# Second slot-routing FFN of a macaron block: its routing written as a table of pieces, emitted among the last stages of the attention, with its transposes done by DMA

## The chip, the cores and the metric

One NeuronCore of a Trainium2 chip runs the whole kernel. The metric is the device time of one execution in microseconds (us); lower is better. A core has five engines that work side by side, each on its own in-order queue: TensorE (PE, matrix products and transposes into PSUM), VectorE (DVE), ScalarE (ACT), GpSimd (POOL) and SyncE (SP, which here only issues transfers). Sixteen DMA engines move data between HBM and the on-chip memory SBUF; SP and ACT issue to them. An engine that waits holds up everything behind it on its queue.

## The reference

Two batches of 4096 tokens with 512 features go through three residual parts, each on a layer norm of its input:

```python
x = x + 0.5 * ffn(layernorm(x))
x = x + attn(layernorm(x))
x = x + 0.5 * ffn(layernorm(x))
```

The attention is a gated delta rule with 16 heads of 32: a 32 x 32 state per head that each token decays, corrects and reads, then an RMS norm, a SiLU gate and an output product. The FFN routes tokens to 64 slots, and the same weights serve both times:

```python
h = gelu(concat(x, mean(S)) @ w1.T + b1)                 # 256 hidden
logits = (h @ w2.T + b2) / (abs(tau) + 0.1)              # 64 slots
alpha = top8_softmax(logits)                             # dense [token, slot], 8 nonzero
slot_input = einsum('bts,btd->bsd', alpha, x) / alpha.sum(1)
S_new = gru(slot_input, S)                               # on 2 x 64 slots only
out = einsum('bts,bsd->btd', alpha, S_new @ wv.T + bv) @ wo.T + bo
```

So an FFN has three stages: a routing over all tokens, a small GRU that needs the routing of every token, and a pass over all tokens that adds alpha times the slot values.

## The kernel before

Tokens are worked on in 32 blocks of 128 positions, both batches together (tiles [128, 2, 512]). The stages in order of time:

1. `ffn_a_phase(..., "a", ...)`: first routing, with the weights' preparation among it, then the first GRU.
2. `attention(...)`: per block, the first FFN's closing product, layer norm, q/k/v/gate projections, triangular solve, a chunked recurrence (`chain`, four chunks of 32 tokens a block, lines 1001 to 1045), and `tail` (norm, gate, output product, residual add at L1083, store to `x2d` in HBM).
3. `ffn_a_phase(..., "c", ...)`: second routing and second GRU (`gru`, L510 on).
4. `after_c`: the closing pass, which adds the second FFN's output to x2 (L641) and stores the result (L642).

The attention is software-pipelined by hand. Each stage of a block is a Python generator that yields after a piece of work, and the table `PIPE` says, in one long line of words such as `chain.2` or `qk0.5*2`, which generator is advanced next and by how many blocks it runs ahead of the loop's step. `run_pipe` walks the table for k from minus the largest lead to 31, under `tc.manual_schedule()`, so each engine gets its instructions in the order of emission. `chain`, `vload`, `tload` and `tail` have leads of 0 to 3; all other stages have done block 31 when step k = 28 ends. The last three steps hold only the recurrence and the tails of the last blocks: the drain.

A routing works on groups of blocks. `split_blocks` makes groups of 1, 4 x 7, 2 and 1 blocks. For each group six generators are entered with start and end times from `PA`, merged by time in `run_merged`, and then ordered by the framework's own scheduler:

- `a_load` loads an x2 block of 512 KB on SP (`load_x2`, L602). The last KEEP = 12 blocks go to tiles that stay until the closing pass (`kx`), the others to XT = 4 rotating tiles (`xt`).
- `a_stats` takes mean and variance on VectorE (L361, L362), then square root (ACT, L365) and reciprocal.
- `a_norm` normalises on VectorE into `xn` (L379, two buffers), casts the high half to fp16 on ScalarE (`xh`, L383), and subtracts on GpSimd for the low half (`xl`, L385). TensorE transposes both halves, 8 + 8 transposes of 128 x 128 into PSUM (L394). ScalarE copies the high half out (`xTh`, L397) and VectorE the low half (`xTl`, L399).
- `a_hidden` makes the hidden layer, 24 matmuls of 256 columns a block (`mm3`, L128 to L130), Gelu on ScalarE (L417), and the logits (L421).
- `a_topk` finds the top 8 of 64 on VectorE with an exponential on ScalarE (L431 to L458) and sums alpha on GpSimd (L461).
- `a_slots` transposes alpha (L472), stores it on chip through `alpha_keep` (L595), and accumulates the slot inputs in PSUM (L480 to L482).

Memory is taken from pools that are opened and closed like a stack. Before, the second routing's pools are opened after the attention's pools and its weights (`aw_es.close()`) are closed. In PSUM (8 banks) the attention holds 2 banks for transposes (`a1t`), 3 for projections (`a1p`), 1 for `pa` and 2 for `pc`.

After the second GRU's weights, 11 x2 tiles (F3X) are loaded for the closing pass; the remaining 9 are loaded in it, on ScalarE's queue (L616).

Of the kernel before, what the change touches and what calls it, by code (L numbers as in the profile page):

```python
# [9 lines left out]
F32 = mybir.dt.float32  # L10
F32R = mybir.dt.float32r
F16 = mybir.dt.float16
# [7 lines left out]
P = 128  # L20
D = 512
# [13 lines left out]
HEAD, TAIL = 1, 1  # L35
CFG = {"a": dict(XT=7, XN=2, XH=10), "c": dict(XT=4, XN=2, XH=11)}
KEEP = 12
F3A, F3X, F3L = 4, 11, 8
# [14 lines left out]
def split_blocks(n):  # L53

    cuts = [0] + list(range(HEAD, n - TAIL, GB)) + [n - TAIL, n]
    cuts = sorted(set(cuts))
    return [(a, b - a) for a, b in zip(cuts, cuts[1:])]
# [17 lines left out]
def run_pipe(tc, stages, n):  # L75


    order = []
    for w in PIPE.split():
        w, _, m = w.partition("*")  # L80
        name, lead = w.split(".")
        order += [(name, int(lead))] * int(m or 1)
    live = {}
    with tc.manual_schedule():
        for k in range(-max(lead for _, lead in order), n):
            for name, lead in order:
                t = k + lead
                if 0 <= t < n:
                    if (name, t) not in live:
                        live[name, t] = stages[name](t)  # L90
                    next(live[name, t], None)
# [3 lines left out]
def tile_macaron(  # L95
# [87 lines left out]
    aw = aw_es.enter_context(tc.tile_pool(name="aw", bufs=1))  # L183
    W = {}
    for n_, cols, dt in (("wqh", NQ, F16), ("wql", NQ, F16), ("wgh", 2 * D, F16), ("wgl", 2 * D, F16),
                         ("wo", D, F32)):
        W[n_] = aw.tile([P, KC, cols], dt, tag=n_, name=n_)
# [121 lines left out]
    def ffn_a_phase(load, adst, nm, extra, before=None, after=None):  # L309

        with tc.tile_pool(name=f"sl{nm}", bufs=1, space=PSUM) as slp, tc.tile_pool(name=f"gp{nm}", bufs=1) as gp:
# [3 lines left out]
            with tc.tile_pool(name=f"f{nm}", bufs=2) as wp, tc.tile_pool(name=f"fs{nm}", bufs=2) as sm, \  # L315
# [3 lines left out]
                groups = split_blocks(NBLK)  # L319
# [4 lines left out]
                for g, (b0, n) in enumerate(groups):  # L324
# [3 lines left out]
                        (t0 - PA["ld"] - n / GB, t1 - PA["ld"] - n / GB, lambda a=args: a_load(*a, load)),  # L328
                        (t0 - PA["st"], t0 - PA["st"] + PA["std"], lambda a=args: a_stats(*a)),
                        (t0, t1, lambda a=args: a_norm(*a)),  # L330
                        (t0 + PA["a2"], t1 + PA["a2"], lambda a=args: a_hidden(*a)),
                        (t1 + PA["a2"], t1 + PA["tk"], lambda a=args: a_topk(*a, wacc)),
                        (t1 + PA["tk"], t1 + PA["tk"] + PA["sl"] * n / GB, lambda a=args: a_slots(*a, adst, sl, ng)),
# [5 lines left out]
            with ExitStack() as es:  # L339
# [3 lines left out]
                if before:  # L343
                    before(es)
                gru(gr, sl, wacc[:, 0:NB], gw, nm)
                if after:
                    after()
# [820 lines left out]
```

## Time and profile before

| | us |
|---|---|
| Median of 3 runs (2350.8 to 2357.18) | 2355.56 |
| The profiled execution, time | 2342.8 |
| The profiled execution, span of the trace | 2341.0 |

| Stage, read from the trace | from (us) | to (us) |
|---|---|---|
| First routing and first GRU | 0 | 303 |
| Attention, to its last solve (L993) | 303 | 1960 |
| Attention, drain to the last residual add (L1083) | 1960 | 2003 |
| Second routing | 2003 | 2250 |
| Second GRU | 2250 | 2283 |
| Closing pass | 2283 | 2341 |

Over the whole span TensorE is busy 90%, VectorE 82%, ScalarE 49% and GpSimd 35%. These are means over stages of very different kinds, so the stages are read one by one: a row of busy times gives, for a stretch of time, each engine's busy us and in brackets its instructions, then the clock that was granted to TensorE (1.00 is full), the busy share of the 16 DMA engines and the GB/s they moved. A line of the timeline gives start, duration, engine, line of the kernel, operation, output and inputs; in square brackets is the idle time of the engine just before, and what ended it. A group line adds count, total busy us, mean ns of one, and the idle time before its instructions. Busy times of TensorE include overlap of pipelined matmuls.

### The profile page before, as it was taken

To read this page: it belongs to the slowest core of one execution; us is meant where nothing else is said; L and a number is where in the kernel's file an instruction comes from. 1 tells how busy PE (TensorE), PEld (TensorE's weight loads), DVE (VectorE), ACT (ScalarE), POOL (GpSimd) and SP (SyncE) were. 2 spreads that over 40 slices of the span, in tenths; PEclk is the share of its full clock that TensorE was granted. 3 is DMA by queue.
4 is the path that set the end of the run, shared out by engine and by line. 5 is a ranking of instruction groups with operands and counts; after the bars stand their busy time and mean duration, and the time that the engine had idled before them with its cause. 6 is when DMAs were issued, how large, how long until landed. Compare 5 with 4: busy or idle time off the path is not lost. (4 is left out here: it accounts for less than half of the span.)

```text
span 2341.0 us, 101047 instructions
## 1 busy us (share of the span) xinstructions
PE 2100.5 (90%) x44989; PEld 1585.4 (68%) x44989; DVE 1911.3 (82%) x4876; ACT 1148.9 (49%) x1957; POOL 808.5 (35%) x750
## 2 busy tenths in 40 slices
PE   5878878999999999999999999999999976588886
PEld 5767757767777676777767677777667754377774
DVE  7898538988888888888889888888888886489656
ACT  4677445544445444444545444554444421367631
POOL 2333114433334343333434333444333441134300
PEclk9898989999999999999999999999999988799997
DMA  6332323344443344343334444344444332630049
GB/s 212 123 127 91 96 87 129 119 133 130 142 134 126 123 136 132 128 150 121 126 124 139 128 136 148 120 127 132 135 128 146 102 97 70 219 110 29 2 149 368
DMA packets 176516, 302.75 MB, mean 129 GB/s; under 512 B 27984, under 2 KB 73552, under 8 KB 176080
## 3 DMA queue, kind: packets, MB, share of 16 engines
q1 hardware_dynamic: 161728, 256.45, 32.9%
q10 hardware_dynamic: 14352, 39.85, 5.2%
q8 instruction: 352, 5.77, 1.2%
q14 instruction: 84, 0.69, 0.1%
HBM read 189.23 MB, written 107.00 MB: 127 GB/s over the span
## 5 line engine op out<-in xcount | busy, mean ns | idle before, releaser
L1080 PE MATMUL apo<-wo,Gt 128*128 128x512 f32 x512 | 279.1, 630 | 24.5 <-DVE x1r L1083 24.5
L128 PE MATMUL pv<-xTh,wgh 128*128 128x256 f16 x1024 | 282.1, 275 | 0.0
L129 PE MATMUL pv<-xTh,wgl 128*128 128x256 f16 x1024 | 280.2, 274 | 0.1
L130 PE MATMUL pv<-xTl,wgh 128*128 128x256 f16 x1024 | 280.3, 274 | 0.0
L1014 POOL TENSOR_TENSOR ps<-ST,AC 128x256 f32<-128x256 f32 x128 | 105.5, 824 | 442.4 <-DVE ST L1038 442.4
L128 PE MATMUL pq<-wqh,xTh 128*128 128x384 f16 (+1 forms) x768 | 242.8, 316 | 1.5 <-issue 0.8
L129 PE MATMUL pq<-wqh,xTl 128*128 128x384 f16 (+1 forms) x768 | 240.9, 314 | 0.2 <-DVE xTl L818 0.2
L130 PE MATMUL pq<-wql,xTh 128*128 128x384 f16 (+1 forms) x768 | 240.7, 313 | 0.0
L862 POOL TENSOR_TENSOR qk<-qk,rn 128x512 f32<-128x512 f32 x128 | 137.6, 1075 | 231.7 <-issue 106.7
L836 ACT ACTIVATE qk<-pq,iscA 128x384 f32<-128x384 f32 (+1 forms) x192 | 105.4, 549 | 162.5 <-PE pq L130 139.5
L980 POOL TENSOR_TENSOR KQ<-KQ,Ax 128x512 f32<-128x512 f32 x128 | 168.4, 1315 | 0.4 <-PE pa L959 0.4
L764 DVE TENSOR_TENSOR tmp<-N,MT 128x256 f32<-128x256 f32 (+7 forms) x384 | 161.2, 426 | 5.6
L758 DVE TENSOR_TENSOR tmp<-N,U 128x256 f32<-128x256 f32 (+7 forms) x384 | 164.0, 434 | 1.4
L838 ACT ACTIVATE sq<-pq,iscA 128x384 f32<-128x384 f32 (+1 forms) x192 | 164.7, 858 | 0.0
L1018 PEld LDWEIGHTS pc<-KQ,S 32*32 32x32 f32 x8192 | 123.2, 106 | 50.6 <-ACT Y L1044 31.0
L760 DVE TENSOR_REDUCE MT<-tmp 128x32 f32<-128x256 f32 (+7 forms) x384 | 153.8, 407 | 0.0
L959 PE MATMUL pa<-KQ 32*32 32x64 f32 x8192 | 143.6, 217 | 11.2 <-ACT KQ L872 4.9
L1018 PE MATMUL pc<-KQ,S 32*32 32x64 f32 x8192 | 142.8, 217 | 9.5 <-DVE S L1040 4.9
L959 PEld LDWEIGHTS pa<-KQ 32*32 32x32 f32 x8192 | 121.7, 105 | 37.9 <-issue 14.9
L1035 PEld LDWEIGHTS pc<-X,u 32*32 32x32 f32 x8192 | 120.7, 105 | 38.6 <-issue 21.9
L1035 PE MATMUL pc<-X,u 32*32 32x64 f32 x8192 | 141.9, 216 | 5.2 <-ACT u L1032 3.7
L917 ACT ACTIVATE vg<-pv,iscA 128x512 f32<-128x512 f32 x128 | 88.1, 688 | 96.7 <-PE pv L130 88.7
(304 smaller groups left out, 5760.3 us busy)
## 6 DMA issues: line engine op xcount, KB each, us to landing
d<-a0d ACTq DMA_DIRECT2D x32, 528.0 KB
Ax<-a0d ACTq DMA_DIRECT2D x32, 528.0 KB
xt<-in_x_dram SPq DMA_DIRECT2D x32, 512.0 KB
x<-in_x_dram SPq DMA_DIRECT2D x64, 256.0 KB
x1d<-x SPq DMA_DIRECT2D x64, 256.0 KB
vtd<-vg SPq DMA_DIRECT2D x64, 256.0 KB
kd<-qk SPq DMA_DIRECT2D x64, 256.0 KB
XK<-kd SPq DMA_DIRECT2D x256, 64.0 KB
```

What stands on the lines that cost most here:

```text
L128: nc.tensor.matmul(po, lh, rh, start=start, stop=False, skip_group_check=True)
L129: nc.tensor.matmul(po, ll, rh, start=False, stop=False, skip_group_check=True)
L130: nc.tensor.matmul(po, lh, rl, start=False, stop=stop, skip_group_check=True)
L758: V.tensor_tensor(tv, vw(f, o10 + j0, [[C, n], [0, h], [1, ni]]), vw(U, ou + j0 * 17, [[0, n], [16, h], [1, ni]]), ALU.mult)
L760: yield lambda tv=tv, j0=j0: V.tensor_reduce(vw(mt, n * j0, [[1, n], [n, h]]), tv, AX.X, ALU.add)
L764: V.tensor_tensor(tv, vw(f, o11 + r0 * C, [[C, h], [0, n], [1, nk]]), vw(mt, 0, [[0, h], [n, n], [1, nk]]), ALU.mult)
L838: nc.scalar.activation(sq[:, f0:f1].rearrange("p (q g e) -> p q e g", g=NG, e=C), pq[:, 0:f1 - f0].rearrange("p (q e g) -> p q e g", g=NG, ...
L959: nc.tensor.matmul(pa[s, m], KQ[s, 0, c, b, g], KQ[s, :, c, b, g], start=(m == 0), stop=True, skip_group_check=True, tile_position=(32 * q ...
L980: nc.gpsimd.tensor_tensor(kc, kc, bass.AP(Ax.tensor, Ax[:, :, c].offset, [list(a[0]), [1, 2], list(a[1]), [1, C]]), ALU.mult)
L1018: nc.tensor.matmul(pcv[s, b, g, 0:2 * C], S[s, b, g], KQ[s, :, c, b, g], start=(g == 0), stop=False, skip_group_check=True, tile_position=tp)
L1035: nc.tensor.matmul(pcv[s, b, g, C:3 * C], u[s, b, g], d["X"][s, :, m], start=False, stop=True, skip_group_check=True, tile_position=tp)
L1080: nc.tensor.matmul(po, Gt[:, k, b], wo[:, k], start=(k == 0), stop=(k == KC - 1))
```

## The change

The second routing gets its own functions; the first keeps the old ones, renamed `fa_...` and `first_routing`. Five things are done:

- A table `ROUTE` orders the second routing's pieces, as `PIPE` orders the attention's, and its emission is fixed by hand. `run_pipe` is split so that a walk through a table (`pieces`) can be advanced step by step.
- When the attention's loop reaches its drain (`now >= drain`, the step after k = 28), the pools of its early stages (`ee`) and its projection weights are closed, `open_c` opens the second routing in that memory, and the walk through `ROUTE` is advanced among the attention's last pieces, from its first step (k = -4) up to `AHEAD` = 1.0 at the attention's end. The rest of the walk follows the attention.
- In `a_norm` two transposing DMA transfers a block, issued on SP, take the place of the TensorE transposes and of the copies out of PSUM. The normalisation is done in place in the `xt` tile, except for the kept blocks.
- The x2 loads are issued on ScalarE's queue. Pools are opened with `reuse_waits="tile"`, by which a new tile waits for the users of the tiles it lies on, not for the whole old pool. The three projection banks of PSUM are shared by attention and routing, which has one bank each for alpha's transposes, logits and slots.
- Numbers: groups of 1, 3, 4 x 6, 3 and 1; XT 6 for 4, XH 8 for 11; KEEP 11 for 12, F3X 12 for 11, F3L 9 for 8.

```diff
-HEAD, TAIL = 1, 1
-CFG = {"a": dict(XT=7, XN=2, XH=10), "c": dict(XT=4, XN=2, XH=11)}
-KEEP = 12
-F3A, F3X, F3L = 4, 11, 8
+HEAD, TAIL = (1, 4), (4, 1)
+CFG = {"a": dict(XT=7, XN=2, XH=10), "c": dict(XT=6, XH=8)}
+KEEP = 11
+
+AHEAD = 1.0
+F3A, F3X, F3L = 4, 12, 9
...
+def pieces(stages, n, table, extra=()):
+
+
+
+    order = leads(table)
+    live = {}
+    heap = [(s0, i, None) for i, (s0, s1, f) in enumerate(extra)]
+    heapq.heapify(heap)
+
+    def others(now):
+        while heap and heap[0][0] <= now:
+            _, i, g = heapq.heappop(heap)
+            s0, s1, f = extra[i]
+            g = g or f()
+            try:
+                heapq.heappush(heap, (s0 + next(g) * (s1 - s0), i, g))
+            except StopIteration:
+                pass
+
+    for k in range(-max(lead for _, lead in order), n):
+        for e, (name, lead) in enumerate(order):
+            others(k + e / len(order))
+            t = k + lead
+            if 0 <= t < n:
+                if (name, t) not in live:
+                    live[name, t] = stages[name](t)
+                next(live[name, t], None)
+                yield k + (e + 1) / len(order)
+    others(n + 1)
+
+
...
+    def route_open(nm, load, adst, extra, side):
+
+        es, fs = ExitStack(), ExitStack()
+        pool = lambda e, name, bufs, **kw: e.enter_context(
+            tc.tile_pool(name=name + nm, bufs=bufs, reuse_waits="tile", side=side, **kw))
+        sl = pool(es, "sl", 1, space=PSUM).tile([P, KC, NB, NS], F32, tag="sl", name=f"sl{nm}")
+        gp = pool(es, "gp", 1)
+        wacc = gp.tile([P, GB * NB, NS], F32, tag="wacc", name=f"wacc{nm}")
+        gw = {}
+        sm, wp = pool(fs, "fs", 2), pool(fs, "f", 2)
+        ptr, ppl = (pool(fs, *a, space=PSUM) for a in (("ft", 1), ("fl", 1)))
+        pools = (wp, sm, ptr, pj3, ppl)
+        groups = split_blocks(NBLK, HEAD, TAIL)
+        ng = len(groups)
+        st = [dict(blocks=(a, b), n=b - a) for a, b in groups]
+        stages = {"load": lambda g: a_load(st[g], g, pools, load),
+                  "stats": lambda g: a_stats(st[g], nm, g, pools),
+                  "norm": lambda g: a_norm(st[g], nm, g, pools),
+                  "hid": lambda g: a_hidden(st[g], nm, g, pools),
+                  "logit": lambda g: a_logits(st[g], nm, g, pools),
+                  "topk": lambda g: a_topk(st[g], nm, g, pools, wacc),
+                  "slots": lambda g: a_slots(st[g], nm, g, pools, adst, sl, ng)}
+        return dict(es=es, fs=fs, sl=sl, groups=groups, wacc=wacc, gw=gw, args=(stages, ng, ROUTE, extra(gp, ptr, gw, ng)))
+
...
+    def a_norm(d, nm, g, pools):
+
+        wp, sm, ptr, ppj, ppl = pools
+        mv, rs = d["mv"], d["rs"]
+        d["xhl"], d["xT"] = [], []
+        for j in range(d["n"]):
+            u = f"{nm}{g}_{j}"
+            xs, xn = d["x"][j]
+            for b in range(NB):
+                i = NB * j + b
+                V.tensor_scalar(xn[:, b], xs[:, b], mv[:, i, 0:1], rs[:, i:i + 1], ALU.subtract, ALU.mult)
+                yield
+            xh = wp.tile([P, NB, D], F16, tag="xh16", name=f"xh{u}", bufs=CFG[nm]["XH"])
+            xl = wp.tile([P, NB, D], F16, tag="xl16", name=f"xl{u}", bufs=CFG[nm]["XH"])
+            d["xhl"].append((xh, xl))
+            xTh = wp.tile([P, NB * KC, P], F16, tag="xTh", name=f"fxTh{u}", bufs=3)
+            xTl = wp.tile([P, NB * KC, P], F16, tag="xTl", name=f"fxTl{u}", bufs=3)
+            d["xT"].append((xTh, xTl))
+            nc.scalar.copy(xh, xn)
+            yield
+            nc.sync.dma_start_transpose(xTh, flat(xh))
+            yield
+            nc.gpsimd.tensor_tensor(xl, xn, xh, ALU.subtract)
+            yield
+            nc.sync.dma_start_transpose(xTl, flat(xl))
+            yield
+
+    def a_hidden(d, nm, g, pools):
+
+        wp, sm, ptr, ppj, ppl = pools
+        d["h"] = []
+        for j in range(d["n"]):
+            u = f"{nm}{g}_{j}"
+            xTh, xTl = (a.rearrange("p (b k) t -> p k b t", b=NB) for a in d["xT"][j])
+            ph = ppj.tile([P, 2, NB * P], F32, tag="pj", name=f"fph{u}")
+            hT = wp.tile([P, 2, NB * P], F32, tag="hT", name=f"hT{u}")
+            d["h"].append(hT)
+            for hc in range(2):
+                for k in range(KC):
+                    hs_ = slice(hc * P, (hc + 1) * P)
+                    mm3(ph[:, hc], w1h[:, k, hs_], w1l[:, k, hs_], xTh[:, k], xTl[:, k], k == 0, k == KC - 1)
+                    if k % 2:
+                        yield
+                nc.scalar.activation(hT[:, hc], ph[:, hc], AF.Gelu, bias=hb[:, hc:hc + 1], scale=isc1)
+                yield
+
...
+    def load_x2(wp, t):
+        if t >= NBLK - KEEP:
+            xt = keep[t] = pk["xk"].tile([P, NB, D], F32, tag=f"x2_{t}", name=f"kx2_{t}")
+            xn = pk["xk"].tile([P, NB, D], F32, tag="xn", name=f"kxn{t}", bufs=2)
+        else:
+            xt = xn = wp.tile([P, NB, D], F32, tag="xt", name=f"xt2_{t}", bufs=CFG["c"]["XT"])
+        nc.scalar.dma_start(xt, x2d[t * P:(t + 1) * P])
+        return xt, xn
+
+    def extra_c(gp, ptr, gw, ng):
+        return [(0.5 * ng, 0.8 * ng, lambda: load_wih(pk["xk"], gw, "c"))]
+
+    def open_c():
+
+        aw_es.close()
+
+        pk["ak"] = kp.enter_context(tc.tile_pool(name="ak", bufs=1, side="right", reuse_waits="tile")).tile(
+            [P, NBLK, NB, P], F16, tag="ak", name="ak")
+        pk["r"] = route_open("c", load_x2, alpha_keep, extra_c, "right")
+        return pieces(*pk["r"]["args"])
+
+    keep = {}
+    rest = attention(tc, nc, locals())
+
+
+    with tc.tile_pool(name="xk", bufs=1, reuse_waits="tile") as xk:
+        pk["xk"] = xk
+        with tc.manual_schedule():
+            for _ in rest:
+                pass
...
-        run_pipe(tc, stages, NBLK)
+        late = ("vload", "chain", "tload", "tail")
+        drain = NBLK - min(lead for name, lead in leads(PIPE) if name not in late)
+        with tc.manual_schedule():
+            for now in pieces(stages, NBLK, PIPE):
+                if now >= drain and rest is None:
+                    ee.close()
+                    rest = open_c()
+                    at = next(rest)
+                    first = at
+                if rest is not None:
+
+                    while at < first + (AHEAD - first) * (now - drain) / (NBLK - drain):
+                        at = next(rest)
+    return rest
...
+ROUTE = """
+    hid.2*2 topk.1*3 hid.2 load.4 topk.1 slots.0 topk.1*3 norm.2 topk.1 norm.2 stats.3 hid.2 norm.2 stats.3 topk.1 hid.2*3
...
+"""
```

`a_load`, `a_stats`, `a_logits`, `a_topk` and `a_slots` of the second routing do the same arithmetic as before, cut into smaller pieces. The drain step is worked out from `PIPE`: 32 minus the smallest lead among the stages other than `vload`, `chain`, `tload` and `tail`, which is 3, so 29.

## The prediction

> **What bounds the kernel now.** I read the 40 slices first (TensorE is full from slice 8 to 32 and thin from 33 on), then the busy time by stretch from where the attention thins out to the end, the timelines of VectorE, TensorE and ScalarE at the seam between attention and second routing, and last, groups and waits inside the second routing.
>
> ```profile
> core 0: us, PE busy (x) PEld busy (x) DVE busy (x) ACT busy (x) POOL busy (x), PEclk, DMA share, GB/s
> 1958.00:2003.00 45.00, 31.22 (x739) 18.12 (x738) 12.12 (x22) 4.30 (x10) 3.83 (x5) 0.78 0.15 48
> 2003.00:2028.00 25.00, 6.21 (x42) 4.63 (x42) 10.65 (x29) 4.78 (x7) 2.64 (x2) 0.59 0.79 288
> 2028.00:2237.00 209.00, 175.78 (x2127) 155.46 (x2127) 166.08 (x460) 144.56 (x195) 78.17 (x39) 0.93 0.18 64
> 2237.00:2250.00 13.00, 9.78 (x203) 8.94 (x200) 8.24 (x38) 7.88 (x14) 2.55 (x5) 0.90 0.01 3
> 2250.00:2283.00 33.00, 28.13 (x164) 22.52 (x162) 16.56 (x47) 5.72 (x15) 0.00 (x0) 0.88 0.75 263
> 2283.00:2341.00 58.00, 35.16 (x118) 23.32 (x116) 37.95 (x62) 10.63 (x28) 0.00 (x0) 0.78 0.97 371
> ```
>
> The rows are six stages: the attention's drain, a gap, the steady second routing, its last groups, the GRU, and the closing pass, which is held by transfers (0.97 of the DMA engines). Drain and gap are 70 us in which VectorE works 23. In the steady routing VectorE (166 of 209) and TensorE (176, overlapped time) are both near full and both wait on the other.
>
> ```profile
> 1957.77 1.86 DVE L993 STREAM_TRANSPOSE TT<-N 128x1024 f32<-128x1024 f32 x1
> 2001.80 0.75 DVE L1083 SCALAR_TENSOR_TENSOR x1r<-apo,rms,x1r 128x512 f32<-128x512 f32 x1 [4.62 <-DMA x1r<-x1d]
> 2012.05 1.29 DVE L361 BATCH_NORM_STATS2 stc<-xt 128x6 f32<-128x512 f32 x2 [9.50 <-DMA xt<-x2d]
> 2019.61 1.03 PE L394 MATMUL fptc<-ident,xhc 128*128 128x128 f16 x8 [19.79 <-ACT xhc L383]
> 2027.15 0.56 ACT L417 ACTIVATE hTc<-fphc,hb,isc 128x256 f32<-128x256 f32 x1 [0.54 <-PE fphc L130]
> ```
>
> The last triangular solve ends at 1959.6, the last residual add at 2002.6; only then do the first x2 tiles load, and the first Gelu comes at 2027. The load, statistics, cast, transpose and first matmuls run one after another.
>
> ```profile
> L379 DVE TENSOR_SCALAR fxnc<-xt,mvc,rsc 128x512 f32<-128x512 f32 x40 | 30.2, 794 | 14.1 <-POOL xlc L385 13.8
> L361 DVE BATCH_NORM_STATS2 stc<-xt 128x6 f32<-128x512 f32 x40 | 25.9, 671 | 9.5 <-DMA xt<-x2d 9.5
> L399 DVE COPY fxTlc<-fptc 128x1024 f16<-128x1024 f16 x32 | 21.7, 677 | 15.2 <-PE fptc L394 15.2
> L362 DVE BATCH_NORM_AGGREGATE mvc<-stc 128x2 f32<-128x6 f32 x64 | 9.9, 164 | 0.0
> ...
> L397 ACT COPY fxThc<-fptc 128x1024 f16<-128x1024 f16 x32 | 32.4, 1011 | 5.7 <-PE fptc L394 5.6
> ```
> ```profile
> DVE fxnc L379 <- POOL xlc L385: 21.2, 7, 4.4
> DVE fxTlc L399 <- PE fptc L394: 15.2, 6, 7.0
> ```
>
> The first answer names what the change takes away (the two copies out of PSUM), the second VectorE's two largest waits in the routing. They are 36 of its 43 us idle there, bar some 4 us of the second that lie in the gap.
>
> **The change, part by part.**
>
> *Routing emitted in the drain.* In the changed program's order on VectorE, 8 statistics, 8 aggregations and 4 normalisations stand ahead of the attention's last residual add: 8 x 0.67 + 8 x 0.16 + 4 x 0.55 (single L379s in the gap take 0.52) = 9 us, about what VectorE does in the gap now (10.65). It idles 33 of the 45 us of the drain, so that work fits. TensorE gets the first block's hidden matmuls, ScalarE one cast and some loads. So after the last residual add the routing should stand where it stands now at 2028: the 25 us go, less what the drain is stretched. The drain is a chain (about 7 us per chunk, from S at L1040 to the next S) in in-order queues. On SP the first transposing transfer, which waits for ScalarE's cast, stands ahead of the store of a last x2 half; the second waits for GpSimd's subtraction (2.13 us, L385) with the last x1 loads behind it, and the last residual adds wait for those. ScalarE's x2 loads (0.3 to 0.4 us an issue on either queue) wait for stores and, later, for GpSimd; casts and evictions queue behind. Bounds of the stretch: 0 (all in idle time) to 20 us (cast, subtraction and a landing of about 4 us twice, for three blocks); I take 5. Gain 20, between 5 and 25.
>
> *Transposes to transfers.* Out go 512 TensorE transposes (8 in 0.62 us when run together at full clock, L394: 40 us in all), 32 ScalarE copies (32.4 us) and 32 VectorE copies (21.7 us, 21.0 of it in the steady stretch). VectorE is the one that counts. With the copies gone their wait goes too (11 us in the stretch). The normalisation now writes into the x tile itself for 21 of 32 blocks, where it had two xn buffers; this takes away the reason for the 21 us behind L385. What waits the fixed table brings instead is in no trace. So the steady stretch becomes between 209 - 21 - 32 = 156 and 209 - 21 = 188 us; I take the middle, 172, where VectorE would be 84% busy against 79% now. Gain 37, between 21 and 53. If that cover fails, ScalarE is next: 144.6 - 32.4 + 32 issues x 0.4 = 125 us.
>
> *Price of a transposing transfer.* 64 of them, 256 KB each, all on SP; none is in this trace. From below: as 128 packets of 2 KB (95 ns each in the trace's packet records) over 16 engines, 0.76 us. From above: cut into 8,192 pieces of 32 bytes at the price of a 128-byte packet (14 ns), 7.3 us. Between: a 128x128 fp16 block is 128 rows of 256 bytes, so 1,024 packets read and as many written at 17.5 ns (the 256-byte row) are 2.2 us. I take this, since runs of 256 bytes are what the shapes give. 64 x 2.2 = 141 us. They can run from about 1990 to 2180 (2237 - 57), so up to 190 / 64 = 3.0 us each is hidden behind VectorE; from 247 / 64 = 3.9 us on they end later than the stage does today.
>
> The Trainium skill (DMA: Bandwidth & Descriptors, Latency and other measured facts) gives 261 GB/s for one measured transposing transfer; by that a transfer would take an estimated 1.0 us and the sum would not change. Against it, VectorE: DVE Perf Modes, The three transpose paths, puts a 128x128 transpose at 1309 ns by DMA and 390 ns by TensorE; eight in a row would be an estimated 10.5 us, and the kernel slower by far. No run so far shows either.
>
> *The rest costs nothing that I can price.* Groups of 1, 3, 4 x 6, 3, 1 blocks for 1, 4 x 7, 2, 1 keep the number of small operations at ten of each. The closing pass still loads 32 - 11 - 12 = 9 tiles late, as now 32 - 12 - 11. Closing pass, GRU and last groups stay at 58, 33 and 13 us. Tile-wise waits on freed memory may spare the attention's start the 3.4 us for its first x load (L788 at 305.9); I leave that out.
>
> *Sum.* -20 - 37 = -57 us. The profiled execution took 2342.8 us (span 2341.0), the median of three runs is 2355.56, 12.8 more; so 2285.8 in that execution's terms, 2298 by the median's. Own range: 2355.6 - 78 = 2278 to 2355.6 - 26 = 2330; with 12 for the seams I left out, 2266.
>
> **Rivals.**
>
> *A. Transfers bind and the kernel gets slower.* From 3.9 us per transfer, SP's stream sets the end of the routing: 1990 + 64 T against 2237. T = 5 gives 2310, +73, 2429; the upper bound 7.3 gives 2457, +220, 2576. For it: 8,192 short pieces are possible, and all 64 stand on one in-order queue with waits on two engines. Against: the shapes allow 256-byte runs, and the DMA engines are 0.18 busy in this stage. The 1309 ns of the skill's page above would be this case. Chance 0.20.
>
> *B. Transfers bind, but below the old time.* T of 3.0 to 3.9, say 3.5: 1990 + 224 = 2214, -23, 2333. Chance 0.08.
>
> *C. The table leaves the idle time as it is.* In-order queues put in the wrong place keep VectorE's 43 us idle, and the drain stretches by 20: -21 - 5 = -26, 2330. For it: the hidden matmuls of a block stand two or three blocks behind its cast, with three transposed buffers, so a late transfer stops TensorE and then VectorE's top-8. Against: ScalarE and TensorE both lose a fifth of their work. Chance 0.10.
>
> *D. It does not do what it says.* If the freed memory comes free only with the attention's last stage, nothing overlaps, and a 20 us stretch of the drain eats the steady gain: 2348 to 2363. The last reader of the freed weights and tiles is the solve at 1959.6, which speaks against it. Chance 0.05.
>
> **How the numbers follow.** The forecast has 0.57, A 0.20, B 0.08, C 0.10, D 0.05. No change means within 0.3% (7 us), about what a measurement can tell. Faster: forecast, B and C, 0.75. D goes mostly to no change, 0.04, and with A to slower, 0.21. Range: 2266 at the lower end leaves out about 0.05; at the upper end A, spread over T from 3.9 to 7.3, leaves some 0.14 above 2430. The likeliest case alone is 2266 to 2330.
>
> **What would show it.** First statistics of the routing before the last residual add, and the first Gelu within 5 us of it (now 25): the overlap. VectorE at 82 to 88% busy in the steady routing, 21 to 24 us per group of four (now 27): the second part. Transfers landing within 3 us of each other while VectorE is the one that is waited for: the price. If instead TensorE waits for transposed tiles in long stretches, A or B is right; if the last residual add comes later than 2020, the drain was mis-sized.

## The result and the profile after

The kernel after takes 2324.4 us (median of four runs, 2319.3 to 2334.5), the kernel before beside it 2353.7 us (four runs). The ratio is 0.986 with a 95% interval of 0.984 to 0.989: faster by 32 us, give or take 6. The forecast was 2298 us, so about half of the expected gain came.

The profiled execution of after is the longest of its four (2334.5 us, span 2332.7), that of before the shortest of its runs (2342.8). The two profiles are therefore only 8 us apart, and stages have to be compared one by one. Busy time by stretch of after, cut at the same events as before (drain, routing with its last groups, GRU, closing pass):

```profile
core 0: us, PE busy (x) PEld busy (x) DVE busy (x) ACT busy (x) POOL busy (x), PEclk, DMA share, GB/s
1974.00:2029.00 55.00, 39.52 (x772) 23.42 (x773) 18.96 (x43) 10.68 (x18) 8.07 (x7) 0.74 0.38 112
2029.00:2241.00 212.00, 158.98 (x1824) 137.36 (x1823) 145.48 (x472) 128.81 (x183) 76.36 (x44) 0.90 0.88 172
2241.00:2274.00 33.00, 28.11 (x153) 22.08 (x153) 15.74 (x46) 3.89 (x9) 0.00 (x0) 0.84 0.47 182
2274.00:2332.70 58.70, 34.20 (x122) 22.05 (x120) 38.38 (x63) 10.95 (x28) 0.00 (x0) 0.80 0.96 367
```

There is no gap row any more. The drain has grown from 43 to 55 us and holds 8 us more of VectorE's work (18.8 against 10.5, cut exactly from the end of the last solve to the end of the last residual add). In the 212 us that follow, VectorE works 145, or 69% (70% up to 2228, without the last groups); the forecast had it at 82 to 88%. The DMA engines, at 0.17 to 0.18 in this stage before, are now at 0.88.

The same seam in the timelines of VectorE and ScalarE (start, duration, engine, line, instruction, and in brackets the idle time ahead of it and what ended it):

```profile
1972.07 1.86 DVE L1232 STREAM_TRANSPOSE TT<-N 128x1024 f32<-128x1024 f32 x1
1986.25 0.68 DVE L393 BATCH_NORM_STATS2 fstc<-xt 128x6 f32<-128x512 f32 x1
2016.97 0.56 ACT L445 ACTIVATE hTc<-fphc,hb,isc 128x256 f32<-128x256 f32 x1
2028.04 0.75 DVE L1323 SCALAR_TENSOR_TENSOR x1r<-apo,rms,x1r 128x512 f32<-128x512 f32 x1 [4.26 <-PE apo L1320]
```

The first statistics now stand 42 us ahead of the last residual add (10 us behind it before), and the first Gelu 11 us ahead of it (25 us behind it before). The overlap does what it says. The last solve ends at 1973.9 against 1959.6; the experiments show that this lies within the spread of the same attention code.

Groups of the routing in after, from 2029 to 2241 (line, engine, operation, count; busy us, mean ns of one; idle time ahead of them and what ended it):

```profile
L393 DVE BATCH_NORM_STATS2 fstc<-xt 128x6 f32<-128x512 f32 x34 | 22.9, 673 | 6.8 <-DMA xt<-x2d 6.8
L412 DVE TENSOR_SCALAR xt<-xt,fmvc,frsc 128x512 f32<-128x512 f32 x38 | 22.6, 644 | 0.0
L399 DVE RECIPROCAL frsc<-frsc 128x8 f32<-128x8 f32 (+2 forms) x8 | 1.6, 195 | 15.4 <-ACT frsc L397 15.4
L464 DVE TENSOR_TENSOR lgc<-plc,b2s 128x512 f32<-128x512 f32 (+2 forms) x10 | 5.7, 572 | 13.5 <-PE plc L454 13.5
L480 DVE SCALAR_TENSOR_TENSOR lgc<-repc,lgc 128x512 f32<-128x512 f32 (+2 forms) x10 | 5.7, 572 | 16.8 <-ACT lgc L478 16.8
```

The copies out of PSUM are gone, and with them their wait; the normalisation into the x tile itself (L412) waits for nothing. But VectorE now waits at three other places, 46 us together: for ScalarE's Sqrt (L397), for TensorE's logits, and for ScalarE's Exp (L478). ScalarE and TensorE are not full, so the question is what they wait for. The waits of SP's queue, TensorE and ScalarE in the same stretch (total, times, longest):

```profile
SPq L422 <- ACT hTc L445: 76.9, 17, 10.1
SPq L422 <- ACT lgc L478: 12.7, 3, 4.7
PE fphc L160 <- DMA fxTlc<-xlc: 22.7, 15, 5.8
PE fphc L158 <- DMA fxThc<-xhc: 12.4, 8, 3.2
ACT hTc L445 <- PE fphc L160: 50.0, 31, 6.2
```

Read as a ring, this says: the Gelu on ScalarE waits for the hidden product, the hidden product waits for transposed tiles, and SP cannot issue the transposing transfers of a later block because the cast that feeds them stands behind that Gelu on ScalarE's in-order queue. The timelines show one stretch of it:

```profile
2104.28 6.25 SPq L422 DMA_TRANSPOSE fxThc<-xhc  x1
2105.34 0.56 ACT L445 ACTIVATE hTc<-fphc,hb,isc 128x256 f32<-128x256 f32 x1 [2.60 <-PE fphc L160]
2105.93 1.28 ACT L478 ACT_TABLE_LOAD   x1
2107.22 0.63 ACT L478 ACTIVATE lgc<-lgc 128x512 f32<-128x512 f32 x1
2107.87 1.28 ACT L445 ACT_TABLE_LOAD   x1
2109.16 0.56 ACT L445 ACTIVATE hTc<-fphc,hb,isc 128x256 f32<-128x256 f32 x1
2109.63 1.03 ACT L420 CAST xhc<-xt 128x1024 f16<-128x1024 f32 x1
2110.96 0.27 PE L158 MATMUL fphc<-fxThc,w1h 128*128 128x256 f16 x1 [3.18 <-DMA fxThc<-xhc]
2113.83 0.56 ACT L445 ACTIVATE hTc<-fphc,hb,isc 128x256 f32<-128x256 f32 x1 [3.17 <-PE fphc L160]
```

SP is held 6.25 us on one transposing transfer (some 1.25 where it is free), the cast of a later block runs only at 2109.63 behind two Gelus, an Exp and the two loads of ScalarE's function table that the change from Gelu to Exp and back brings (1.28 us each), and TensorE stands 3.18 us for a tile. Two limits show here, and only one is the ring. The tile that TensorE waits for is that of the transfer at 2104.28: its cast had ended at 2102.02, and what took the time was SP's queue and the transfer itself. Of the 32 transfers of high halves in after, 18 are issued within 0.1 us of the end of their cast; the other 14 find the cast done, and are issued 0.1 to 0.2 us after SP comes free from the transfer before. The DMA engines' load over 2090 to 2125, in 40 slices of 0.9 us, tenths of full:

```profile
DMA  6992004869197999999999779999989929049599
```

The transfers come in bursts: nothing around 2094, close to full from 2100 to 2117. The low halves that lie on the chain of waits in this stage land 5.3 to 8.7 us after they are issued (seven of eight; the other 3.7), although the mean load leaves room.

### The profile page after: what moved, and what is told of

Its sections match the earlier page's. It is cut to its first block, busy times and chain, and to the rows that moved or that the text cites. A ratio compares the mean times of both kernels' runs of the same rounds, so it can differ in the third digit from the quotient of the medians.

```text
span 2332.7 us, 100069 instructions
## 1 busy us (share of the span) xinstructions
PE 2079.5 (89%) x44477; PEld 1560.9 (67%) x44477; DVE 1881.8 (81%) x4844; ACT 1125.2 (48%) x1928; POOL 806.2 (35%) x750
## 3 DMA queue, kind: packets, MB, share of 16 engines
q1 hardware_dynamic: 224848, 256.98, 36.2%
## 4 chain that ended last, share of the span: by engine, by line
PE 63%; DVE 15%; DMA 12%; issue 4%; ACT 3%; POOL 1%; SPq 1%; ACTq 0%; DVEq 0%; POOLq 0%
PE apo L1320 9%; PE pa L1197 5%; PE pv L158 5%; PE pc L1274 5%; PE pc L1257 4%; PE pv L159 4%; PE pv L160 4%; PE pq L158 4%; DMA kd<-qk 4%; PE pq L159 4%; PE pq L160 4%; PE pc L1267 3%; DMA x1r<-x1d 2%; DMA fxTlc<-xlc 2%; PE kqt L1107 2%
## 5 line engine op out<-in xcount | busy, mean ns | idle before, releaser
L1003 DVE TENSOR_REDUCE N<-tmp 128x32 f32<-128x128 f32 (+4 forms) x320 | 135.3, 423 | 0.0
```

## The experiments

Twelve kernels. In the table "drain" runs from the end of the last solve to the end of the last residual add, "to GRU" from there to the first instruction of the GRU on VectorE, both from each kernel's one profile. The ratio is that to the kernel before, run on the same chip beside it.

| kernel | median us | ratio (95%) | drain | to GRU | sum |
|---|---|---|---|---|---|
| before | 2353.7 to 2357.2 | 1 | 42.9 | 248.3 | 291.3 |
| after | 2324.4 | 0.9862 (0.9835–0.9889) | 54.9 | 212.3 | 267.2 |
| b_dma | 2325.3 | 0.9870 (0.9848–0.9891) | 42.2 | 222.0 | 264.2 |
| e_noahead | 2328.7 | 0.9891 (0.9864–0.9918) | 46.4 | 228.2 | 274.6 |
| e_halfT | 2305.4 | 0.9793 (0.9769–0.9818) | 51.2 | 193.4 | 244.6 |
| e_3T | 2353.0 | 0.9989 (0.9967–1.0010) | 53.2 | 225.3 | 278.5 |
| e_strict | 2343.5 | 0.9936 (0.9914–0.9958) | 42.9 | 238.8 | 281.7 |
| e_bothPE | 2347.5 | 0.9952 (0.9933–0.9970) | 48.3 | 241.4 | 289.7 |
| e_xlPE | 2333.6 | 0.9906 (0.9884–0.9927) | 51.1 | 222.1 | 273.2 |
| b_xhPE | 2333.8 | 0.9904 (0.9886–0.9921) | 42.2 | 227.2 | 269.4 |
| e_castDVE | 2332.8 | 0.9910 (0.9891–0.9928) | 51.5 | 220.7 | 272.2 |
| e_castPOOL | 2313.0 | 0.9825 (0.9805–0.9846) | 52.2 | 197.2 | 249.4 |
| e_plan | 2342.3 | 0.9951 (0.9928–0.9974) | 54.9 | 227.9 | 282.8 |
| b_few | 2331.8 | 0.9908 (0.9874–0.9941) | 43.1 | 226.0 | 269.1 |

### b_dma: only the transfers, in the old order

```diff
             nc.gpsimd.tensor_tensor(xl, xn, xh, ALU.subtract)
             yield (j + 0.4) / blocks[1]
+            if nm == "c":
+                xTh = wp.tile([P, NB * KC, P], F16, tag="xTh", name=f"fxTh{u}", bufs=3)
+                xTl = wp.tile([P, NB * KC, P], F16, tag="xTl", name=f"fxTl{u}", bufs=3)
...
+                nc.sync.dma_start_transpose(xTh, flat(xh))
...
+                nc.sync.dma_start_transpose(xTl, flat(xl))
...
+                continue
```

> The kernel before, with one edit: in the second routing the 16 TensorE transposes and two copies of a block give way to two transposing transfers on SP; order, memory and the seam to the attention stay. Theory (transfers cost about 1.84 us of all DMA engines each, 64 x 1.84 = 118 us, hidden under a 209 us stretch when nothing else is compressed): VectorE's 21 us of copies come free, 10 to 25 us faster than before, 2330 to 2345 us. Rival (a transfer that waits on SP for ScalarE and GpSimd holds the x2 loads behind it on the same queue): no gain, 2350 to 2375. Its attention is the old one: if its last triangular solve ends at 1958 to 1962, the 14 us by which the attention ended later in the profile after belong to the change; if it ends at 1965 or later, they are variation between executions.

Measured 2325.3 us, below the range of its theory (2330 to 2345) and as fast as the whole change: 31 us off the kernel before. Busy time by stretch of this kernel (drain, gap up to the first Gelu, routing up to the GRU):

```profile
core 0: us, PE busy (x) PEld busy (x) DVE busy (x) ACT busy (x) POOL busy (x), PEclk, DMA share, GB/s
1969.10:2011.30 42.20, 28.71 (x738) 16.98 (x738) 10.50 (x22) 4.29 (x10) 3.83 (x5) 0.84 0.16 52
2011.30:2037.80 26.50, 5.25 (x24) 3.41 (x24) 10.76 (x29) 4.93 (x7) 5.51 (x4) 0.55 0.84 284
2037.80:2233.30 195.50, 157.84 (x1834) 137.11 (x1834) 152.85 (x466) 115.94 (x173) 75.66 (x43) 0.90 0.69 152
```

From first Gelu to GRU it takes 195.5 us; before takes 223.7 (2027.2 to 2250.9), after 224.1 (2017.0 to 2241.1). So the transfers alone bring 28 us there, and the rest of the change loses the same 28 us in this stage and gets it back at the seam. The attention is the old one here, and its last solve ends at 1969.1; in the profiles of this table with the old attention that end lies at 1959.6, 1967.9, 1969.1 and 1974.3, with the new one at 1962.0 to 1973.9. The 14 us by which it is later in the profile after lie within that spread.

### e_noahead and e_strict: the overlap

```diff
-AHEAD = 1.0
+AHEAD = -10.0
```

> The kernel after, but the routing's pieces are held back until the attention's last piece is out (only its first x2 load goes ahead). Theory (the stretch of the drain from 43 to 55 us is the routing's own work among the attention's): last solve to last residual add returns to 43 to 46 us, the gap of some 20 to 25 us to the first Gelu comes back, so the time is 8 to 15 us above after, 2332 to 2340. Rival (the drain is longer because memory and PSUM are shared or waits are tile-wise): the drain stays at 53 to 56 us and the time is 20 to 27 us above after, 2345 to 2352.

This run did not do what its expectation says: the scheduler merged the two stretches whose order is written out, and statistics of the first blocks still ran in the drain (the first at 1979.5, the last residual add at 2017.5); only TensorE's hidden products stayed behind the attention's last output products (the first at 2015.2). The time, 2328.7, can't be told from after. It was made again so that no queue mixes:

```diff
             for now in pieces(stages, NBLK, PIPE):
                 if now >= drain and rest is None:
...
-                if rest is not None:
-                    while at < first + (AHEAD - first) * (now - drain) / (NBLK - drain):
-                        at = next(rest)
+            while at < AHEAD:
+                at = next(rest)
```

> The kernel after, with the same routing pieces that it emits among the attention's last steps emitted right behind the attention's last piece instead, so that no engine's queue mixes the two. Theory (the overlap is worth the gap of 20 to 25 us less the 12 us by which it stretches the drain): last solve to last residual add 43 to 46 us, first Gelu 20 to 25 us behind it, time 8 to 15 us above after, 2332 to 2340. Rival (what the overlap brings is taken back in the routing, since transfers hold its pace and start no sooner): within 6 us of after, 2318 to 2331.

```profile
core 0: us, PE busy (x) PEld busy (x) DVE busy (x) ACT busy (x) POOL busy (x), PEclk, DMA share, GB/s
1963.60:2006.50 42.90, 30.34 (x738) 17.46 (x738) 10.49 (x21) 4.29 (x10) 3.82 (x5) 0.82 0.18 63
2006.50:2020.70 14.20, 2.90 (x12) 1.75 (x13) 7.61 (x19) 2.65 (x4) 2.12 (x1) 0.50 0.60 172
2020.70:2245.30 224.60, 167.05 (x1846) 143.13 (x1845) 145.07 (x475) 132.37 (x188) 78.49 (x45) 0.85 0.85 168
```

The drain is back at 43 us, so its stretch to 55 is the routing's work among the attention's. Behind it come 14 us to the first Gelu (20 to 25 were expected; the first loads of x2 are already issued) and 224.6 us to the GRU, as after has (224.1). The time is 19 us above after, where 8 to 15 were expected: the overlap is worth 17 to 19 us (the ratios give 0.9936 - 0.9862 = 0.0074 of 2355), or 14.5 by the stages of the two profiles (281.7 against 267.2). The rival, that the routing takes it back, falls.

### e_halfT and e_3T: fewer and more transfers

```diff
-            xTl = wp.tile([P, NB * KC, P], F16, tag="xTl", name=f"fxTl{u}", bufs=3)
-            d["xT"].append((xTh, xTl))
+            d["xT"].append((xTh, xTh))
...
-            nc.sync.dma_start_transpose(xTl, flat(xl))
```

> The kernel after with only one transposing transfer a block: the transpose of the low half is left out and the high half stands in for it, so the low part of the routing's hidden product is left out of what is computed. Theory (DMA engines near full in the second routing, 0.87, so transposed tiles land 5 to 8 us after issue, and TensorE and then VectorE wait): from last residual add to GRU 212 falls to 180 to 195 us, VectorE goes above 75% busy there, time 2292 to 2312. Rival (the in-order table leaves the idle time, not the transfers): 205 to 213 us, time 2316 to 2328.

```diff
             nc.sync.dma_start_transpose(xTl, flat(xl))
+            xTe = wp.tile([P, NB * KC, P], F16, tag="xTe", name=f"fxTe{u}", bufs=1)
+            nc.sync.dma_start_transpose(xTe, flat(xh))
```

> The kernel after with a third transposing transfer a block, of the high half once more into a tile that nobody reads. Theory (DMA engines near full): 32 x 1.84 = 59 us of more engine time against some 13% of 200 us that are free, so 30 to 59 us slower than after, 2354 to 2384. Rival (the in-order table sets the pace, transfers are hidden): within 8 us of after, 2317 to 2332.

With 32 transfers fewer 193 us from last residual add to GRU instead of 212, and 2305 us; with 32 more 225 us, 2353 us, and the whole gain gone. The first agrees with its theory, the second stays just under its range of 2354 to 2384. A transfer costs between 0.6 (19 / 32) and 0.9 us (28.6 / 32) of the kernel's time: less than the engines spend on it, but it is not hidden. This is the price of a transfer with what hangs on it, and not of the DMA engines alone: each also takes 1.2 us or more of SP's queue, and e_halfT frees the hidden product from waiting for GpSimd's subtraction (2.1 us a block).

### e_bothPE, e_xlPE and b_xhPE: the transposes back on TensorE, whole or half

In e_bothPE both transfers go, and ahead of a block's hidden product (or, where its half tiles are ready, behind the first half of the product before it) stands

```diff
+        for w in range(2):
+            xw = flat(d["xhl"][j][w])
+            pt = pools[3].tile([P, NB * KC, P], F16, tag="pj", name=f"fpt{nm}{g}_{j}_{w}")
+            for i in range(NB * KC):
+                nc.tensor.transpose(pt[:, i], xw[:, i * P:(i + 1) * P], ident16)
+            if w:
+                V.tensor_copy(d["xT"][j][1], pt)
+            else:
+                nc.scalar.copy(d["xT"][j][0], pt)
```

> The kernel after with its table and its overlap, but with the transposes back on TensorE (16 a block, ahead of the block's hidden product) and their copies on ScalarE (high half) and VectorE (low half). Theory (the transfers alone brought the 28 us, and table and overlap are worth 0 to 12 us): 2340 to 2358. Rival (table and overlap bring some 25 us by themselves, and the DMA engines' load takes that back in the kernel after): 2312 to 2332.

In e_xlPE the high half's transfer stays:

```diff
-            nc.sync.dma_start_transpose(xTl, flat(xl))
...
+        pt = pools[3].tile([P, NB * KC, P], F16, tag="pj", name=f"fpt{nm}{g}_{j}")
+        for i in range(NB * KC):
+            nc.tensor.transpose(pt[:, i], xl[:, i * P:(i + 1) * P], ident16)
+        if j % 2:
+            V.tensor_copy(d["xT"][j][1], pt)
+        else:
+            nc.scalar.copy(d["xT"][j][1], pt)
```

> The kernel after with the high half's transpose left as a transfer and the low half's put back on TensorE (8 transposes, 0.62 us a block), its copy by turns on ScalarE (1.01 us) and VectorE (0.68 us). Theory (64 transfers bring the DMA engines to 0.88 in the routing; 32 leave them at 0.56, and then TensorE, at 0.75 of the time, has room for 20 us more): 2305 to 2318. Rival (the in-order table sets the pace, so added work on three engines only adds): 2326 to 2345.

And in the kernel before, with the low half alone by transfer:

```diff
+            if nm == "c":
+                xq = wp.tile([P, NB * KC, P], F16, tag="xTl", name=f"fxTl{u}", bufs=3)
+                nc.sync.dma_start_transpose(xq, flat(xl))
...
+                if nm == "c" and eng == 1:
+                    continue
```

> The kernel before with one transposing transfer a block, of the low half, so that VectorE's copies go; the high half's transposes stay on TensorE and its copies on ScalarE. Theory (in the old order VectorE was the bound, so its 21 us of copies are the gain, and the load of the DMA engines costs little there): 2318 to 2330, as with both halves by transfer (2325). Rival (ScalarE's copies or the DMA load matter as much): 2335 to 2350 if the copies, 2300 to 2315 if the load.

Table and overlap without transfers give 2347.5 us, by the ratio 11 us below the kernel before, as the theory said. Table, overlap and half of the transfers give 2333.6, between the two and 9 us above after: the DMA engines are down to 0.58 in the routing, but TensorE, ScalarE and VectorE have 13, 15 and 6 us more to do, and that weighs more. The theory of this run (2305 to 2318) falls; the time lies in the range of its rival, by which added work only adds. In the old order a half share of transfers gives 2333.8, 8.5 us above the full share: the theory (2318 to 2330) is missed, and there too ScalarE's copies cost more than the DMA load, though not quite as much as the rival said (2335).

### e_castDVE and e_castPOOL: the cast off ScalarE's queue

```diff
-            nc.scalar.copy(xh, xn)
+            V.tensor_copy(xh, xn)
```

> The kernel after with one instruction a block moved: the cast of the normalised tile to its high fp16 half goes from ScalarE to VectorE, right behind the normalisation that feeds it. Theory (a ring of waits: a Gelu waits for TensorE, TensorE for a transposed tile, SP's transfer for the cast, and the cast stands behind the Gelu in ScalarE's queue; SP waits 98 us for ScalarE in the routing): SP's waits for ScalarE disappear, last residual add to GRU falls from 212 to 185 to 200 us although VectorE gets some 30 us more, time 2298 to 2313. Rival (the DMA engines, 0.88 busy, set the pace, and VectorE's extra work adds): 210 to 225 us, time 2320 to 2338.

```diff
-            nc.scalar.copy(xh, xn)
+            nc.gpsimd.tensor_copy(xh, xn)
```

> As the run before it, with the cast on GpSimd, just ahead of the subtraction there, at 1 to 2.1 us a block. Theory (the ring of waits): GpSimd has the room (76 of 212 us busy), SP's waits for ScalarE go, last residual add to GRU 185 to 200 us, time 2295 to 2313. Rival (DMA engines): 205 to 215 us, 2318 to 2328. Third (a cast and a subtraction in a row on GpSimd put 3 to 4 us on each block's path): 215 to 235 us, 2327 to 2350.

On VectorE the cast gains nothing: 220.7 us to the GRU and 2332.8 us, both in the range of the rival, with VectorE at 183.7 us of work; SP now waits 63.4 us for the cast there. On GpSimd it takes 2313.0 us, as its theory said (2295 to 2313), and below both kernels: 41 us under before. Its stretch from last residual add to GRU, and below it what VectorE and GpSimd show there:

```profile
core 0: us, PE busy (x) PEld busy (x) DVE busy (x) ACT busy (x) POOL busy (x), PEclk, DMA share, GB/s
1967.20:2019.30 52.10, 37.56 (x772) 22.50 (x773) 18.58 (x43) 9.40 (x17) 10.15 (x9) 0.79 0.40 129
2019.30:2216.50 197.20, 152.67 (x1826) 134.86 (x1823) 161.62 (x473) 99.46 (x153) 109.11 (x74) 0.93 0.81 183
```
```profile
L412 DVE TENSOR_SCALAR xt<-xt,fmvc,frsc 128x512 f32<-128x512 f32 x38 | 30.5, 850 | 0.0
L480 DVE SCALAR_TENSOR_TENSOR lgc<-repc,lgc 128x512 f32<-128x512 f32 (+2 forms) x10 | 14.4, 1442 | 10.1 <-ACT lgc L478 10.1
L399 DVE RECIPROCAL frsc<-frsc 128x8 f32<-128x8 f32 (+2 forms) x8 | 1.3, 167 | 0.5 <-ACT frsc L397 0.5
L420 POOL CAST xhc<-xt 128x1024 f16<-128x1024 f32 x19 | 21.3, 1123 | 44.6 <-PE slc L522 23.6 <-DVE xt L412 15.5 <-PE fphc L160 3.3
```
```profile
PE fphc L160 <- DMA fxTlc<-xlc: 15.7, 9, 5.0
PE fphc L158 <- DMA fxThc<-xhc: 1.8, 3, 0.7
```

TensorE's wait for transposed tiles falls from 35 to 17.5 us, and VectorE's wait for the Sqrt from 15.4 to 0.5, with the same 64 transfers. So the DMA engines' rate alone was not the bound; ScalarE was part of it. The run takes two things off ScalarE at once, the cast's place behind the Gelus and its 1.04 us a block of work (ScalarE is busy 99 us in the stage instead of 129), and no run separates them; that ScalarE has idle time in both speaks for the place. SP still waits long (53 us for GpSimd's cast): that wait by itself was a poor sign to look for. What the cast now waits for is the next limit: 24 us of its idle time in this group end with a slots product (L522) that gives a half tile free.

### e_plan and b_few: the table, or the memory

```diff
-        with tc.manual_schedule():
-            for _ in rest:
-                pass
+        for _ in rest:
+            pass
```

> The kernel after with its overlap as it is, but the routing behind the attention's last piece no longer held to the table's order: the scheduler that orders the rest of the kernel before orders it, in the same memory and with the same transfers. Theory (the table's fixed order is what costs: first Gelu to GRU takes 224 us with it, 195 us in the old order with the same transfers): 195 to 212 us, time 2296 to 2314. Rival (fewer buffers set it: 8 against 11 pairs of half tiles, one bank for the logits against two): 215 to 228 us, time 2316 to 2335.

And to b_dma:

```diff
-CFG = {"a": dict(XT=7, XN=2, XH=10), "c": dict(XT=4, XN=2, XH=11)}
+CFG = {"a": dict(XT=7, XN=2, XH=10), "c": dict(XT=4, XN=2, XH=8)}
...
-                    tc.tile_pool(name=f"fl{nm}", bufs=2, space=PSUM) as ppl:
+                    tc.tile_pool(name=f"fl{nm}", bufs=2 if nm == "a" else 1, space=PSUM) as ppl:
```

> The kernel before with both transposes by transfer (as in the first run), and with the second routing's buffers cut to those that the kernel after has: 8 instead of 11 pairs of half tiles, one PSUM bank instead of two for the logits, one instead of three for the transposed weights of the slots (it gets one more, three, for the hidden products, as after has). Theory (the fewer buffers are the price of doing it while the attention still holds its memory): first Gelu to GRU goes from 195 us to 210 to 226, time 2340 to 2357. Rival (the buffers are enough, and what makes the routing 224 us in the kernel after is the order on ScalarE, SP and TensorE): 193 to 203 us, time 2320 to 2333.

Leaving the routing's order to the scheduler makes it slower (2342.3; from first Gelu to GRU 239.7 us), outside the ranges of both theory and rival, so a written order is not the fault as such. Cutting the buffers in the old order costs 3.7 us in the stage (199.2 against 195.5) and 6.5 us in the medians, whose ratios' intervals overlap; the stage is in the range of its rival (193 to 203). So of the 28.6 us between the two routings with the same transfers (224.1 and 195.5) the buffers explain some 4, and the cast on ScalarE some 16 by the profiles (224.1 against 208.0, 2008.5 to 2216.5, with the cast on GpSimd), or 9 to 11 by the times of whole kernels. If these parts add, some 9 us or more stay unexplained. One candidate is in the traces and was not tried: from first Gelu to GRU ScalarE loads its function table for Gelu, Sqrt or Exp 38 times in after (and in e_castPOOL) and 30 times in b_dma, at 1.28 us each; that is 10 us more on the engine that the ring goes through. The other groups, the loads on ScalarE's queue and the normalisation in place were not tried alone either.

## Why the prediction was right in direction and too large

**Where the time fell.** 2324 us lies in the forecast's own range (2266 to 2330), but near its slow end and not by its mechanism: the steady routing, which was to give two thirds of the gain, gave none in the whole change. That the time is in the range is in part luck.

**Overlap (forecast -20, from 5 to 25): right in size.** 17 to 19 us by the times of e_strict, 14.5 by the stages. Both parts of the working were off and cancel in part, so the nearness to 20 is in part luck. The drain is stretched by 12 us, not 5, since TensorE's queue holds the first hidden products, which wait for transfers, ahead of the attention's last output products. In after the chain of waits runs from the first block's low half to these products:

```profile
2006.53 2.13 POOL xlc L424
2008.69 4.59 DMA fxTlc<-xlc
2022.51 5.51 PE apo L1320 x8
```

In e_noahead, where the hidden products stand behind the output products, the stretch is 3.5 us. And the first Gelu does not follow the last residual add but stands 11 us ahead of it, where without the overlap it stands 14 us behind (e_strict).

**Transposes by transfer in the steady routing (209 to 172, -37): the term that failed.** The removal itself is worth what the working said, a little less: 28 us in the old order. What failed is the sentence that chose the value: "What waits the fixed table brings instead is in no trace", after which the middle was taken. What comes with the table (its order, fewer buffers, other groups, loads on ScalarE's queue, the normalisation in place) brings 29 us to the stage, so that from first Gelu to GRU it takes 224 us with or without the overlap, as long as before the change. The cast on ScalarE is 9 to 16 of the 29 and the buffers some 4; the cause of the rest stays open. The sum in the runs' terms, by the ratios: -31 (transfers, before to b_dma), +16 (what comes with the table, b_dma to e_strict; 17.5 by the stages, 281.7 against 264.2), -17 (overlap, e_strict to after): -32. These are steps along one row of kernels, so they add up by construction.

**Rival C was the nearest.** It said that in-order queues in the wrong place keep VectorE's 43 us idle and stretch the drain, that a late transfer stops TensorE and then VectorE's top-8, and gave 2330. VectorE's idle time in the stretch became 66 us (212 - 145.5). The argument against it, that ScalarE and TensorE lose a fifth of their work, was no argument: both have idle time, but the cast stands behind a Gelu whatever the load. C's other part, 20 us of stretch in the drain, came with 12. It was given 0.10 and deserved more, since the order of two instructions on ScalarE could be read from the changed program.

**Price of a transposing transfer (2.2 us taken, 0.76 to 7.3 the bounds): right in size, by luck.** In the page's table of queues, SP's queue has 67,584 packets and 16.8 MB more in after than in e_bothPE, which differs by the 64 transfers, and 36.2% against 30.6% of 16 engines' span: (844 - 719) / 64 = 1.96 us each; before and b_dma give (871 - 770) / 64 = 1.6 in the same way. The packets are of 256 bytes, as the working assumed, but their number and price were not: the records hold 1,024 a transfer, not 2,048, and each took 29 ns in the mean, not 17.5. The two errors nearly cancel. Rivals A and B, in which that price sets the end, did not come: 2.0 is below 3.0, and e_castPOOL does the stage with the same transfers in 15 us less. But "hidden behind VectorE" was wrong too: e_halfT and e_3T put 0.6 to 0.9 us of each on the time. The landings were forecast within 3 us and took 5 to 9 where they counted.

**The signs named in advance.** VectorE at 82 to 88% did not come (69%), a group of four took 24.9 us in the mean (22.5 to 27.8 between the L480 of two groups; 26.5 in the mean before) instead of 21 to 24, and the last residual add came at 2028.8, past the 2020 named as the mark of a mis-sized drain; 12 us of the 26 by which it is later are the drain, the rest the spread of the attention. "TensorE waits for transposed tiles" came too, with 35 us, and would have been misread: it was named as the sign of A or B, and it is as well the sign of transfers that are issued late.

The Trainium skill (VectorE: DVE Perf Modes, The three transpose paths) puts a 128x128 transpose by DMA at 1309 ns. Eight such blocks go in one transfer here, at 1.96 / 8 = 0.25 us of the engines' time each, and even the landings on the chain, 3.7 to 8.7 us after the issue, stay below the 10.5 us of eight in a row; so the measurement decides against using that figure for a long row of blocks. The Trainium skill's other figure, 261 GB/s (DMA: Bandwidth & Descriptors, Latency and other measured facts), compares with 256 KB in 1.96 us, 134 GB/s, here beside other traffic.

**The rest costs nothing: right, within 2 us.** GRU 31.1 to 32.8, closing pass 59.0 to 58.8 us.

## What to carry to other kernels

When work moves off a full engine, look at the in-order queue that feeds its replacement: here the cast that starts each transfer stood behind activations that waited for earlier transfers, and moving it to the engine with room gave 9 to 11 us that the removed copies had not. Before two changes are added up, price each alone: transfers alone made all of the gain, the overlap another 17 us or so, and what came with the table that both were written in took some 16 back. A DMA share near 0.9 did not mean that the rate alone was the bound; the same bytes went in 7% less time with the cast on another engine.

## What was not expected of the hardware

VectorE's instructions got longer where they met GpSimd's subtraction. One such meeting in e_castPOOL, and below it the same instruction in after:

```profile
2073.37 2.13 POOL L424 TENSOR_TENSOR xlc<-xt,xhc 128x1024 f16<-128x1024 f32 x1
2073.66 2.38 DVE L480 SCALAR_TENSOR_TENSOR lgc<-repc,lgc 128x512 f32<-128x512 f32 x1
```
```profile
2084.85 0.66 DVE L480 SCALAR_TENSOR_TENSOR lgc<-repc,lgc 128x512 f32<-128x512 f32 x1
```

Five of the six L480 of this size start during a subtraction in e_castPOOL. They take 2.37 to 2.50 us, and each ends 0.54 to 0.56 us after the subtraction; in after none meets one, and they take 0.66 to 0.69. So the mean of all L480 goes from 572 to 1442 ns, and that of L412 from 644 to 850, while statistics (673 and 671) and the top-8 searches (213 and 213) did not change. VectorE thus has 161.6 us of work in e_castPOOL where it has 145.5 in after, for the same instructions. The cast on GpSimd is not what does it: in e_castDVE, where GpSimd has the same work as in after, five L480 take 2.07 us and end the same 0.55 us after a subtraction, and L412 takes 805 ns. What the edits move is when the two meet. The Trainium skill (GPSIMD Engine Reference, Specifications) says that GpSimd's way to SBUF is shared with VectorE, with contention for VectorE's instructions with two SBUF inputs or in a two-port mode. L480, which reads two SBUF tensors, agrees.

SP itself is held while it issues a transposing transfer: 1.23 us at the least, 6.25 us at the most in after, where it comes on full engines. In b_dma and e_castPOOL, with the same 64 transfers, the longest is 2.88 and 2.82 us. And the same attention code ended its last solve up to 15 us apart in the profiles of four kernels (1959.6 to 1974.3).
